# The last eight rows go tile to tile into the first quarter of the columns at two seams

## The chip, the cores and the metric

The kernel runs on one core of one Trainium2 chip. The metric is the device time of one execution in microseconds (us). In the profile PE is the matmul engine (PEld its weight loads), DVE the vector engine, ACT the scalar engine, POOL the GpSimd engine and SP the sync engine, which computes nothing and only issues DMAs. ACT and POOL issue DMAs too; a "q" behind an engine's name (SPq, ACTq) marks its sequencer, which issues and waits.

## The reference

Two layers follow each other. Each normalises a tensor x of 32 images, 48 channels, 64 rows and 128 columns (group norm), and adds to x the result of four scans. In a scan each row (or column) is the input's row plus a convolution of five taps over the row before it, so its steps can't run side by side.

```python
def step(w, b):
    def f(carry, inp):
        nxt = inp + _conv1d(carry, w, b)
        return (nxt, nxt)
    return f
...
x = x + _L0_conv_ref(_gn(x), ...)   # rows down, rows up, columns right, columns left
x = x + _L1_conv_ref(_gn(x), ...)
```

## The kernel before

The 32 images are four groups of eight. A rows phase takes one group through 63 steps down and 63 steps up. A columns phase takes a pair of groups through 127 steps right and 127 left. `PHASES` lists twelve phases, one after the other: eight of rows, four of columns. A step is nine products of matrices on PE (`step`, L741) into three tiles of PSUM, each of which DVE evicts into the big tile `arena` (L750).

The arena holds three slots. In a rows phase the rows 0 to 31 lie in one slot and the rows 32 to 63 in another; a partition is a channel and the column modulo 8. In a columns phase a slot holds a quarter of the columns (32 of them) for both groups of the pair; a partition is a channel and the row modulo 8. So what one row leaves in one partition must go to other partitions, and this goes through DRAM: `move_rows` (L589) writes eight rows to the tensor `upa` or `upb` in ten DMAs, all of whose runs are 32 elements (128 bytes) long, and `load_unit` (L633) reads a sixth of a quarter, in runs of up to 2048 elements.

Where a columns phase follows the rows phase of its own pair (`follows`), the rows leave the last scan just before the columns need them. That is so at two places, here called the seams: from phase 1 to phase 2 and from phase 5 to phase 6. In the upward scan row 0 comes last, and the first quarter of the columns, in the slot that the rows phase leaves free, needs all 64 rows before the first columns step. The second quarter is needed by step 32, the third by step 64, and so on.

The order is written out by hand: `at(t, fn, ...)` puts a call on an agenda at a time counted in steps, and `in_order` chains each engine's instructions in the order in which they were traced. SP issues the DMAs in this order, except those given to another queue. At a seam, with t0 the first step of the columns:

- `plan_rows` cuts the rows into eights, the last eight into two and six (`cuts`, L865 to L868): rows 8 to 15 are written when row 8 is done, rows 2 to 7 when row 2 is done, rows 0 and 1 when row 0 is done.
- `plan_cols` loads the first quarter of the group just scanned on POOL's queue, in five parts of the rows (L897 to L901). The last two parts are rows 2 to 7 and rows 0 and 1.
- `hold_queues` (L648) at t0 + 1.2 makes SP and ACT wait for the first columns step: SP by a DMA of one element of each of the 128 partitions into a DRAM tensor `pin`, ACT by a copy.
- the second quarter is loaded behind it, half of its units on ACT, half on SP (L907), then on SP the third quarter (L910), the spill of the first (L911) and the fourth (L912).

Each DMA of SP and ACT takes the next of eight semaphores in traced order, and waits until the DMA that had this semaphore before, the eighth before it, has landed.

Of the kernel before, what the change touches and what calls it, by code (L numbers as in the profile page):

```python
# [43 lines left out]
E8 = 8  # L44
FULL = 128
NG = E8 * C // FULL
NQ = 4
# [3 lines left out]
PIECES = (  # L51
    (0, 0, 48, 0, 0),
    (1, 0, 48, 0, 48),
    (2, 0, 32, 0, 96),
    (2, 32, 48, 1, 0),
    (3, 0, 48, 1, 16),
    (4, 0, 48, 1, 64),
    (5, 0, 16, 1, 112),
    (6, 0, 48, 2, 0),
# [61 lines left out]
def kernel(  # L121
# [8 lines left out]
    nc = tc.nc  # L130
    B, _, H, W = x.shape
# [5 lines left out]
    RUN = KQ * GB  # L137
# [73 lines left out]
        for half in range(2)  # L211
    }

    def by_row(t, e, h0, h1):


        t = t.rearrange("c (i q a e n) -> e a c i q n", i=E8, q=NQ, a=NH, e=E8)[e, h0 // E8]
        return t[:, h0 % E8 : h0 % E8 + h1 - h0].rearrange("c i q n -> c (i q) n")

    def lines(t, h0, h1):  # L220

# [3 lines left out]
    def by_col(t, e, j):  # L225


        return t.rearrange("c (i q n) -> i q c n", i=E8, q=NQ)[e, j]

    def dma(dst, src, queue=None):  # L230
        (queue or nc.sync).dma_start(dst, src)

    tail = {}

    def in_order(fn, *args):


        traced = nc.cur_bb.bb.instructions
        n = len(traced)
        fn(*args)  # L240
        for ins in traced[n:]:
            if ins.engine in tail:
                tc.add_manual_dep(
                    ins,
                    tail[ins.engine].name,
                    mybir.DependencyInfo(
                        mybir.DependencyClass.NoSync, mybir.DependencyReason.DATA
                    ),
                    reason="in_order",
                )  # L250
            tail[ins.engine] = ins

    def pieces(o):
        return [(e, c0, c1, p0) for e, c0, c1, g, p0 in PIECES if g == o]
# [3 lines left out]
    def slots(k):  # L258

        return (0, 1, 2) if k % 2 == 0 else (2, 1, 0)  # L260
# [322 lines left out]
    def row_views(k):  # L583
        return [slot[i].rearrange("p (o h n) -> p o h n", o=NG, h=HALF) for i in slots(k)]

    def row(k, h):
        return row_views(k)[h // HALF][:, :, h % HALF]

    def move_rows(k, h0, h1, to_dram):  # L589

        _, layer, g = PHASES[k]
        view = row_views(k)[h0 // HALF]
        t = (ups if to_dram else source)[layer][g]
        for h in range(h0, h1, E8):
            end = min(h1, h + E8)
            for o in range(NG):
                for e, c0, c1, p0 in pieces(o):
                    here = view[p0 : p0 + c1 - c0, o, h % HALF : h % HALF + end - h]
                    here = here.rearrange("p h (q n) -> p (h q) n", q=NQ)
                    there = by_row(t, e, h, end)[c0:c1]  # L600
                    if to_dram:
                        dma(there, here)
                    else:
                        dma(here, there)
# [25 lines left out]
    def quarter(k, j):  # L630
        return slot[slots(k)[j % 3]].rearrange("p (o s n) -> p s o n", s=2, o=NG)

    def load_unit(k, j, i, a0=0, a1=NH, e0=0, e1=E8, queue=None):  # L633


        _, layer, pair = PHASES[k]
        o, half = UNITS[i]
        part = slice(a0 * LINE, a1 * LINE)
        for e, c0, c1, p0 in pieces(o):
            if not e0 <= e < e1:  # L640
                continue
            dma(
                quarter(k, j)[p0 : p0 + c1 - c0, half, o, part],
                by_col(ups[layer][2 * pair + half], e, j)[c0:c1, part],
                queue,
            )

    def hold_queues(k):  # L648

        done = quarter(k, 0)[:, 0, 0, RUN : RUN + 1]  # L650
        dma(pin, done)
        nc.scalar.copy(junk[:, BN - 1 :], done)
# [167 lines left out]
    def at(t, fn, *args):  # L820
        agenda.append((t, len(agenda), fn, args))
# [31 lines left out]
    def plan_rows(k, t0, prev):  # L853
        if k == 1:
            ahead, scaled = (-34, -18, -3, 12), (-12, -2, 17, 33)
        elif prev == "cols":
            ahead, scaled = (-28, -12, 4, 20), (-13, 3, 19, 35)
        else:
            ahead, scaled = (-54, -43, 0, 11), (-22, -8, 16, 30)
        if k:  # L860
            for i in range(4):
                at(t0 + ahead[i], move_rows, k, i * LOAD, (i + 1) * LOAD, False)
                at(t0 + scaled[i], scale_rows, k, i * LOAD, (i + 1) * LOAD)

        cuts = list(range(0, H + 1, E8))  # L865
        following = PHASES[k + 1][0] == "cols"
        if following and follows(k + 1):
            cuts = [0, E8 // 4] + cuts[1:]  # L868
        for h0, h1 in zip(cuts, cuts[1:]):
            t = t0 + 2 * (H - 1) - h0  # L870
            if k == 0:
                t += 16 if h0 >= HALF else 68
            elif not following:
                t = t0 + 92 + 5 * (H - h1) / E8 + (34 if h1 <= HALF else 0)
            at(t, move_rows, k, h0, h1, True)
        at(
            t0 + H - 1,
            nc.gpsimd.tensor_copy,
            last.rearrange("p (o n) -> p o n", o=NG),
            row(k, H - 1),  # L880
        )

    def follows(k):

        _, layer, pair = PHASES[k]
        return PHASES[k - 1] == ("rows", layer, 2 * pair + 1)

    def plan_cols(k, t0, prev):
        _, layer, pair = PHASES[k]
        n = 2 * NG  # L890
# [3 lines left out]
        for i in range(n):  # L894
            if follows(k) and UNITS[i][1] == 1:
                other = nc.gpsimd
                at(t0 - 31 + i, load_unit, k, 0, i, 4, NH, 0, E8, other)  # L897
                at(t0 - 13 + i, load_unit, k, 0, i, 2, 4, 0, E8, other)
                at(t0 - 6 + i / n, load_unit, k, 0, i, 1, 2, 0, E8, other)
                at(t0 - 1.5, load_unit, k, 0, i, 0, 1, E8 // 4, E8, other)  # L900
                at(t0, load_unit, k, 0, i, 0, 1, 0, E8 // 4, other)  # L901
            else:
                early = 30 if after else 46 if k == 2 else 70
                at(t0 - early + 2 * i, load_unit, k, 0, i)
            if follows(k):
                queue = nc.scalar if i % 2 else nc.sync
                at(t0 + 1.5, load_unit, k, 1, i, 0, NH, 0, E8, queue)  # L907
            else:
                at(t0 + (3 if after else -24 + 2 * i), load_unit, k, 1, i)
            at(t0 + (38 if after else 8) + 2 * i, load_unit, k, 2, i)  # L910
            at(t0 + 33 + 2 * i, spill_unit, k, i, False)  # L911
            at(t0 + 50 + 2 * i, load_unit, k, 3, i)  # L912
        final = k == len(PHASES) - 1
        left = t0 + W - 1
        end = left + W - 1
        for i in range(n):

            t = left + 64 + 2 * i if layer == 0 else left + 39.5 + 4.5 * i
# [13 lines left out]
        n = len(tiles)  # L932
        direct = [u for u in units if not (final and u[1] == 0)]

        for u, (t, j, i) in enumerate(direct):
            nat = tiles[u % n]
            o, half = UNITS[i]
# [26 lines left out]
        if layer == 0:  # L964
            t = units[-1][0] + 14
# [30 lines left out]
    for k, (kind, layer, _) in enumerate(PHASES):  # L996
        (plan_rows if kind == "rows" else plan_cols)(k, starts[k], PHASES[k - 1][0])
# [26 lines left out]
    def first_group():  # L1024
# [80 lines left out]
        for b in range(GB):  # L1105
            stats.take(NBN // 2, parts[1], b)
            stats.aggregate(b)
        move_rows(0, 8, 16, False)
        for r in range(0, 8, 2):
            permute_rows(1, r, r + 2, free, nc.gpsimd)  # L1110
# [22 lines left out]
        take_in(1, 0, nats1[0])  # L1133

    in_order(first_group)
    at(starts[0] + 10, scale_rows, 0, 40, 48)
    for j in range(1, 4):
# [7 lines left out]
    def catch_up(t):  # L1145
        while agenda and agenda[0][0] <= t:
            _, _, fn, args = agenda.pop(0)
            in_order(fn, *args)

    for k in range(len(PHASES)):  # L1150
        for one in scans(k):
            catch_up(done)
            in_order(one)
            done += 1
# [54 lines left out]
```

## Time and profile before

| | |
|---|---|
| median of three runs | 4293.07 us (4291.05 to 4299.52) |
| the profiled execution's own time | 4290.3 us |
| its span, first to last instruction | 4288.2 us |
| PE busy | 4058.9 us (95%) |
| wait of the first columns step, first seam | 14.1 us |
| the same, second seam | 14.4 us |

The wait rows are from the view of who waited for whom. The steps between them run without a gap on PE, some 1.96 us each, so time is won or lost where PE stops. Other stops (at the start, and at the seam of the two last columns phases) are not touched by the change.

### The profile page before, as it was taken

To read this page: it belongs to the slowest core of one execution; us is meant where nothing else is said; L and a number is where in the kernel's file an instruction comes from. 1 tells how busy PE (TensorE), PEld (TensorE's weight loads), DVE (VectorE), ACT (ScalarE), POOL (GpSimd) and SP (SyncE) were. 2 spreads that over 40 slices of the span, in tenths; PEclk is the share of its full clock that TensorE was granted. 3 is DMA by queue.
4 is the path that set the end of the run, shared out by engine and by line. 5 is a ranking of instruction groups with operands and counts; after the bars stand their busy time and mean duration, and the time that the engine had idled before them with its cause. 6 is when DMAs were issued, how large, how long until landed. Compare 5 with 4: busy or idle time off the path is not lost. (4 is left out here: it accounts for less than half of the span.)

```text
span 4288.2 us, 89979 instructions
## 1 busy us (share of the span) xinstructions
PE 4058.9 (95%) x36648; PEld 4029.3 (94%) x36648; DVE 2164.5 (50%) x6503; ACT 1340.1 (31%) x2662; POOL 886.2 (21%) x906
## 2 busy tenths in 40 slices
PE   3699998999999999998999999999999999999992
PEld 1699998999999999998999999999999999999992
DVE  6345444446664444444446654444444444444443
ACT  1584301435793564100006772613000002210122
POOL 4271001325323020010005310000000024510352
PEclk9899999999999999999999999999999999999996
DMA  9599799857998979679308979939289049999999
GB/s 213 113 216 162 105 167 168 245 127 213 230 198 156 163 140 160 103 127 206 85 1 242 222 154 149 148 50 161 43 140 200 1 78 247 247 243 156 180 202 182
DMA packets 2116733, 680.12 MB, mean 159 GB/s; under 512 B 2005440, under 2 KB 2056160, under 8 KB 2076384
## 3 DMA queue, kind: packets, MB, share of 16 engines
q1 hardware_dynamic: 2015904, 581.64, 70.2%
q10 hardware_dynamic: 97216, 86.44, 9.9%
q0 software_dynamic: 3200, 6.30, 0.5%
q8 instruction: 288, 4.72, 0.5%
q14 instruction: 125, 1.02, 0.1%
HBM read 397.38 MB, written 295.98 MB: 162 GB/s over the span
## 5 line engine op out<-in xcount | busy, mean ns | idle before, releaser
L614 ACT ACTIVATE arena<-arena,offset,scale 128x256 f32<-128x256 f32 (+2 forms) x816 | 575.6, 801 | 432.9 <-DMA arena<-mid 176.1
L673 POOL TENSOR_TENSOR arena<-arena 128x2048 f32<-128x2048 f32 x80 | 363.1, 4553 | 1386.0 <-PE step_10l L741 434.1
L569 POOL COPY arena<-arena 96x256 f32<-96x256 f32 x448 | 265.0, 650 | 553.8 <-DMA arena<-in_x 444.2
L512 ACT ACTIVATE early<-arena 128x256 f32<-128x256 f32 x192 | 129.4, 674 | 477.2 <-POOL arena L673 471.2
L741 PE MATMUL step_00r<-arena,early 128*128 128x128 f32 x2286 | 251.5, 274 | 14.1 <-DMA arena<-upa 14.1
L741 PEld LDWEIGHTS step_00r<-arena,early 128*128 128x128 f32 x2286 | 251.1, 185 | 14.5 <-issue 14.4
L741 PE MATMUL step_01r<-arena,early 128*128 128x128 f32 x2286 | 250.6, 273 | 14.4 <-DMA arena<-upa 14.4
L741 PEld LDWEIGHTS step_01r<-arena,early 128*128 128x128 f32 x2286 | 250.4, 185 | 14.6 <-issue 14.5
L741 PE MATMUL step_11r<-arena,early 128*128 128x128 f32 x2286 | 251.3, 273 | 8.2 <-DVE arena L750 8.2
L741 PEld LDWEIGHTS step_11r<-arena,early 128*128 128x128 f32 x2286 | 250.8, 185 | 8.7 <-DVE arena L750 8.6
L741 PE MATMUL step_00l<-arena,wleft 128*128 128x128 f32 x2286 | 249.1, 272 | 0.0
L741 PEld LDWEIGHTS step_00l<-arena,wleft 128*128 128x128 f32 x2286 | 248.6, 184 | 0.0
L741 PE MATMUL step_10l<-arena,wleft 128*128 128x128 f32 x2286 | 248.5, 272 | 0.0
L741 PE MATMUL step_11l<-arena,wleft 128*128 128x128 f32 x2286 | 248.5, 272 | 0.0
L741 PE MATMUL step_01l<-arena,wleft 128*128 128x128 f32 x2286 | 248.4, 272 | 0.0
L741 PE MATMUL step_10r<-arena,early 128*128 128x128 f32 x2286 | 248.4, 272 | 0.0
L741 PEld LDWEIGHTS step_10l<-arena,wleft 128*128 128x128 f32 x2286 | 248.4, 184 | 0.0
L741 PEld LDWEIGHTS step_11l<-arena,wleft 128*128 128x128 f32 x2286 | 248.4, 184 | 0.0
L741 PEld LDWEIGHTS step_01l<-arena,wleft 128*128 128x128 f32 x2286 | 248.4, 184 | 0.0
L741 PEld LDWEIGHTS step_10r<-arena,early 128*128 128x128 f32 x2286 | 248.4, 184 | 0.0
L698 ACT COPY arena<-arena 128x256 f32<-128x256 f32 x172 | 99.7, 656 | 411.5 <-POOL arena L673 162.2
L240 ACT COPY early<-arena 128x1 f32<-128x1 f32 x2 | 0.4, 191 | 657.9 <-DVE arena L750 657.9
(189 smaller groups left out, 7171.3 us busy)
## 6 DMA issues: line engine op xcount, KB each, us to landing
arena<-in_x SPq DMA_DIRECT2D x24, 1536.0 KB, 11.6
xin<-arena SPq DMA_DIRECT2D x96, 384.0 KB, 4.7
arena<-xin SPq DMA_DIRECT2D x96, 384.0 KB, 8.5
mid<-arena SPq DMA_DIRECT2D x96, 384.0 KB, 7.8
arena<-mid SPq DMA_DIRECT2D x192, 192.0 KB, 4.2
upb<-arena SPq DMA_DIRECT2D x192, 192.0 KB, 3.9
arena<-upb SPq DMA_DIRECT2D x96, 384.0 KB, 12.3
arena<-xin SPq DMA_DIRECT2D x186, 192.0 KB, 4.3
```

What stands on the lines that cost most here:

```text
L240: fn(*args)
L512: nc.scalar.activation(junk[:, 0:n], view[:, b], AF.Identity, accum_out=self.sum[:, i, j : j + 1])
L569: copy(dst[:, r, q], src[:, r0 + r, q])
L614: nc.scalar.activation(args[0], args[0], AF.Identity, bias=args[2], scale=args[1])
L673: eng.tensor_tensor(unit, unit, nat, ALU.add)
L698: copy(by_w(perm)[:, a], src[:, a])
L741: nc.tensor.matmul(part(whole(ps[o])[0:m], -s), weights[:, i, at : at + m], part(src(i), s), start=seen[o] == 1, stop=seen[o] == left[o],)
```

## The change

`send_row` copies one row's first quarter of columns straight from the rows' slot into the first quarter's slot of the columns phase, in one DMA for each piece of the channels that lies together on both sides: 94 DMAs a seam, of 16 to 48 partitions and 128 bytes a partition. They alternate between ACT and SP. For columns 0 to 3 modulo 8 a row is sent when it is done (47 DMAs over eight rows); for columns 4 to 7 all eight rows are sent after the last row, by `send_rest` (47 DMAs). `together` chains these DMAs over the two queues in traced order.

`move_rows` gets a form that writes the first quarter of the columns alone (`nq=1`): this is what goes to DRAM of rows 8 to 15 before the seam. Rows 0 to 7 and 8 to 15 are written in full at t0 + 1.3, which is behind `hold_queues` and ahead of the loads of the second quarter. The loads of rows 0 to 7 by POOL fall away.

```diff
+    def send_row(k, h, wanted):
+        here = row(k - 1, h)
+        for e, c0, c1, o, p0 in PIECES:
+            if e not in wanted:
+                continue
+            for i, d0, d1, to, q0 in PIECES:
+                a, b = max(c0, d0), min(c1, d1)
+                if i != h or a >= b:
+                    continue
+                turns[0] += 1
+                dma(
+                    quarter(k, 0)[q0 + a - d0 : q0 + b - d0, 1, to, e * RUN : (e + 1) * RUN],
+                    here[p0 + a - c0 : p0 + b - c0, o, 0:RUN],
+                    nc.scalar if turns[0] % 2 else nc.sync,
+                )
+
+    def send_rest(k, wanted):
+        for e in wanted:
+            for h in range(E8 - 1, -1, -1):
+                send_row(k, h, (e,))
+
+    together += [send_row, send_rest]
...
-        if following and follows(k + 1):
-            cuts = [0, E8 // 4] + cuts[1:]
+        seam = following and follows(k + 1)
+        if seam:
+            cuts = cuts[2:]
+            end = t0 + 2 * (H - 1)
+            at(end - E8, move_rows, k, E8, 2 * E8, True, 1)
+            for h in range(E8 - 1, -1, -1):
+                at(end - h, send_row, k + 1, h, range(0, E8 // 2))
+            at(end, send_rest, k + 1, range(E8 // 2, E8))
+            at(end + 1.3, move_rows, k, 0, E8, True)
+            at(end + 1.3, move_rows, k, E8, 2 * E8, True)
...
-                at(t0 - 1.5, load_unit, k, 0, i, 0, 1, E8 // 4, E8, other)
-                at(t0, load_unit, k, 0, i, 0, 1, 0, E8 // 4, other)
```

More of the change, by code (lines that the diff above doesn't have):

```diff
@@ L212, with by_row @@
     }
-    def by_row(t, e, h0, h1):
+    def by_row(t, e, h0, h1, nq):
         t = t.rearrange("c (i q a e n) -> e a c i q n", i=E8, q=NQ, a=NH, e=E8)[e, h0 // E8]
-        return t[:, h0 % E8 : h0 % E8 + h1 - h0].rearrange("c i q n -> c (i q) n")
+        t = t[:, h0 % E8 : h0 % E8 + h1 - h0]
+        return t.rearrange("c i q n -> c (i q) n") if nq == NQ else t[:, :, 0]
     def lines(t, h0, h1):
@@ L233 @@
     tail = {}
+    queues = (nc.sync.engine, nc.scalar.engine)
+    together = []
     def in_order(fn, *args):
@@ L250, in in_order @@
                 )
+            if ins.engine in queues and "DMA" in ins.opcode:
+                if fn in together and "queue" in tail:
+                    tc.add_manual_dep(
+                        ins,
+                        tail["queue"].name,
+                        mybir.DependencyInfo(
+                            mybir.DependencyClass.NoSync, mybir.DependencyReason.DATA
+                        ),
+                        reason="together",
+                    )
+                tail["queue"] = ins
             tail[ins.engine] = ins
@@ L587, in row, with move_rows @@
         return row_views(k)[h // HALF][:, :, h % HALF]
-    def move_rows(k, h0, h1, to_dram):
+    def move_rows(k, h0, h1, to_dram, nq=NQ):
         _, layer, g = PHASES[k]
@@ L598, in move_rows @@
                     here = view[p0 : p0 + c1 - c0, o, h % HALF : h % HALF + end - h]
-                    here = here.rearrange("p h (q n) -> p (h q) n", q=NQ)
-                    there = by_row(t, e, h, end)[c0:c1]
+                    there = by_row(t, e, h, end, nq)[c0:c1]
+                    if nq == NQ:
+                        here = here.rearrange("p h (q n) -> p (h q) n", q=NQ)
+                    else:
+                        here = here[:, :, 0:RUN]
                     if to_dram:
@@ L646, in load_unit @@
             )
+    turns = [0]
+    def send_row(k, h, wanted):
[12 more added lines that the diff above has]
+                    nc.scalar if turns[0] % 2 else nc.sync,
+                )
+    def send_rest(k, wanted):
[3 more added lines that the diff above has]
+    together += [send_row, send_rest]
     def hold_queues(k):
```

## The prediction

> **What bounds the kernel now.** PE is busy 95% of the span, so I went to the view of who waited for whom on PE and took the waits that the change can reach:
>
> ```profile
> PE step_01r L741 <- DMA arena<-upa: 14.4, 1, 14.4
> PE step_00r L741 <- DMA arena<-upa: 14.1, 1, 14.1
> ```
>
> Each is one wait, the first columns step at a seam. The timeline of the first seam shows what it waits for:
>
> ```profile
> 654.44 5.16 SPq L231 DMA_DIRECT2D upa<-arena  x10
> 657.50 3.94 POOL L231 DMA_DIRECT2D arena<-upa  x8 [3.22 <-DMA upa<-arena]
> 662.19 1.00 POOL L231 DMA_DIRECT2D arena<-upa  x2 [0.74 <-issue]
> 665.29 24.97 PE L741 MATMUL step_00r<-arena,early 128*128 128x128 f32 x200 [14.10 <-DMA arena<-upa]
> 668.34 0.35 SPq L231 DMA_DIRECT2D pin<-arena  x1
> 668.77 19.67 ACTq L231 DMA_DIRECT2D arena<-upa  x6
> 668.78 20.10 SPq L231 DMA_DIRECT2D arena<-upa  x6
> ```
>
> The last row's eviction ends at 651.59 (call this T). Its write starts only at 654.44, since SP still issues rows 2 to 7; the loads by POOL run till 664.7. Then SP sends the pin DMA, and both queues start on the second quarter. Step 1's last eviction ends at 670.01, that is T + 18.42, where an ordinary step takes 1.96. Of the 16.46 lost, 14.10 is PE idle and 2.36 is the slow clock behind it. The busy time by stretches shows that clock, and something else:
>
> ```profile
> 654.00:665.00 11.00, 0.00 (x0) 0.00 (x0) 0.00 (x0) 0.00 (x0) 5.22 (x11) 0.50 0.63 115
> 665.00:671.00 6.00, 5.71 (x27) 5.58 (x27) 1.05 (x3) 0.19 (x1) 0.00 (x0) 0.50 0.73 21
> 671.00:677.00 6.00, 6.00 (x58) 6.00 (x57) 2.88 (x9) 0.00 (x0) 0.00 (x0) 1.00 0.69 31
> 677.00:717.00 40.00, 39.98 (x369) 39.91 (x368) 19.66 (x62) 0.00 (x0) 0.00 (x0) 1.00 0.98 171
> ```
>
> The last three columns are granted clock, DMA share and GB/s. From 668 to 676 the DMA engines are held but move 21 to 31 GB/s, against 171 later. That stretch is the pin DMA's life; the list of issues has it at 8.1 us to landing for half a kilobyte:
>
> ```profile
> pin<-arena SPq DMA_DIRECT2D x1, 0.5 KB, 8.1
> ```
>
> At the second seam pin is issued at 1946.31 and 8 KB packets become short again at 1954.8: the same 8.5. I read it as 128 writes of 4 bytes to one place that hold up all that is behind them.
>
> The second quarter's loads end at 716.7 (last issue 703.6, 12.9 to landing); at the second seam at 1990.2. They are needed by step 32, DVE's row with the longer 0.65:
>
> ```profile
> 730.25 0.65 DVE L750 SCALAR_TENSOR_TENSOR arena<-step_00r,bd,arena 128x128 f32<-128x128 f32 x2 [0.72 <-PE step_00r L741]
> 731.14 0.35 DVE L750 SCALAR_TENSOR_TENSOR arena<-step_00r,bd,arena 128x128 f32<-128x128 f32 x1 [0.23 <-PE step_00r L741]
> ```
>
> So step 32 ends at 731.49 = T + 79.9, with 14 us of slack on its loads. At the second seam T is 1929.35 and step 32 ends at 2008.63, T + 79.3, with 17 us of slack. The change eats this slack from both ends: the steps come earlier, the loads later. Last, the price of 128-byte packets, from the DMA view of 618 to 630, where rows are written and little else runs:
>
> ```profile
> DMA packets 14970, 1.95 MB, mean 162 GB/s; under 512 B 14959, under 2 KB 14959, under 8 KB 14969
> q1 hardware_dynamic: 14952, 1.89, 100.7%
> ```
>
> 14952 packets in 12 us at a full share: 1246 packets per us.
>
> **What goes at the start of the columns.** The write and read of rows 0 to 7 leave the path. Row 0's five pieces for columns 0 to 3 are issued within 1 to 2 us of T. Tile-to-tile copies are not in this trace; the nearest rows are the smallest row writes here, at 1.6 to 2.0 from issue to landing, as an upper end the 4.0 of a 192 KB row write. I take 1.8, since these pieces are smaller than either. Step 1 then starts near T + 1.5 to 3 in place of T + 13.7, and step 32 would end near T + 65 if nothing else held it: 15 us better. The pieces for columns 4 to 7 land in the order in which steps 4 to 7 want them; the worst is 1 or 2 us late. The added waits on PE's first eight steps are some tenths each. All this is hidden if step 32 stalls anyway, so the next part decides.
>
> **What comes on the path: the second quarter.** Its loads read whole channels of the group just scanned, so they must follow the full write of rows 0 to 15, which now stands behind hold_queues, which stands behind 47 pieces on SP. Queued behind the same writes: on ACT its ten loads (its statistics start only at 728.2, and wait for an input load that is late too); on SP the other ten, the third quarter, an input load, the spills. Counted from T at the first seam:
> - Send_rest: 47 pieces on two queues, 24 on one. SP's ten issues in 5.16 us are 0.52 each: 12.5, starting 0.6 after T. Pin is issued at T + 13.1. If the eight semaphores bind instead, with 4.0 to landing, it is 47 x 4.0 / 8 = 23.5; with the 1.8 taken they don't (10.6).
> - Pin holds the engines for 8.1: T + 21.2. Bounds: nothing, if 128-byte writes pass where 8 KB reads did not, and 8.5. I take all of it, as both queues stood still under it at both seams.
> - Two blocks of rows, 8 x 384 x 4 x 2 = 24576 packets at 1246 per us: 19.7. T + 40.9. The last landing 2.0 later (1.6 to 4.0): T + 42.9. In the trace of before most of this ran ahead of the seam, beside row steps.
> - The loads: before they took from pin's landing at 676.4 to 716.7, 40.3, and 1.2 for what had passed under pin: 41.5. T + 84.4. Bounds: 31.3, if 6.29 MB go at the 201 GB/s of 710 to 720, and 45.
> - Step 32's evictions 1.0: T + 85.4. It has waited over 20 us, so I add the slow clock behind such a wait, 2.4 as at the seam: T + 87.8.
>
> Against T + 79.9 that is 7.9 lost. At the second seam the loads took 1954.8 to 1990.2, with 1.2 for the rest 36.6: 42.9 + 36.6 + 3.4 = T + 82.9 against T + 79.3, 3.6 lost. Together 11.5. The first quarter of rows 8 to 15 written twice is within these packets; written ahead it is 3072 packets, 2.5 us in a stretch that now has room, at no cost on PE while POOL's loads of these rows end before T (they take 5 us of the 16). SP's later work starts about 17 us later; the fourth quarter's loads at the first seam landed at 832, 28 before use, so I count nothing there.
>
> The profiled execution took 4290.3, its span 4288.2, the median is 4293.07. 4290.3 + 11.5 = 4301.8; the median carried over gives 4304.6, and I say 4304. About 0.2%, 8.6 us, is what a measurement of this kernel can tell from no change.
>
> **Two rules beside the rows.** The Trainium skill, "TensorE: Matmul & The Clock Gate", section "Part 1: The HAM clock gate", has the full clock back after some 3.4 us of sustained work, where the row shows half clock for 5.7 us after PE resumed; by the rule the term would be 1.7, the total 1.4 us less. The Trainium skill, "DMA: Bandwidth & Descriptors", section "Bandwidth", advises against just such small pieces (below 64 KB the descriptors dominate), and its section "Anatomy of one DMA" has a fixed 2.0 us for each; an estimate from that page is 47 x 2.0 / 8 = 11.8 in place of 12.5. No run here shows such a piece yet.
>
> **The rivals.**
> - *Pin holds nothing back.* [...] Against: even the other queue's packets stood. Each seam is 8.1 better, together 11.5 - 16.2 = -4.7: 4288, no change to be told.
> - *Faster: the second quarter comes in time.* If pin holds nothing and the loads run at 201 GB/s, the seams come to T + 66.1 + 3.4 = 69.5: 10.4 and 9.8 won, 4273. From loads landed by about T + 64 on, the whole 14 to 15 a seam is won: 4264. For: alone on the engines, loads do reach that rate at 710. Against: 159 to 184 GB/s from 680 to 710 with two queues reading, as here.
> - *Slower still: the pieces bind.* With 4.0 to landing, 11 more a seam: 4326. For: the writes beside full engines show it. Against: the engines are nearly idle just then.
>
> That the chain over two queues does not hold is hardly open: in the built program ACT and SP each have 47 pieces, in turn, and pin behind them.
>
> **How the numbers follow.** Forecast 0.52, pin holds nothing 0.20, faster 0.20, pieces bind 0.08. The forecast's own bounds (issue at 0.44 instead of 0.52, loads 3 either way, landing) are about 9 either way, 4295 to 4313, and reach into "same" with a tenth; the second case spreads into "faster" a little. So slower 0.54, same 0.23, faster 0.23. The range 4272 to 4322 leaves out the full gain and the worst of the last case.
>
> **What would show it.** Right: PE's wait of 14 gone or under 4 at the seams, and in its place one wait of 15 to 25 at step 32, on DMA arena<-upa; ACT's ten loads issued from T + 43; few GB/s in the 8 us behind pin. Wrong: no wait at step 32 (the gain stands), writes at full rate right behind pin (second case), or pin issued after T + 20 (last case).

## The result, and the profile after

The changed kernel takes 4316.9 us (median of five, 4310.94 to 4323.94), beside 4294.43 for the kernel before (4291.05 to 4299.52): a ratio of 1.0051, 95% interval 1.0035 to 1.0066. It is slower by some 22 us, twice what was forecast. Its profiled execution took 4312.47, with a span of 4310.7.

Again the view of who waited for whom on PE comes first (in all, times, longest):

```profile
PE step_00r L785 <- DVE arena L794: 17.2, 2, 16.3
PE step_01r L785 <- DVE arena L794: 15.9, 2, 14.0
PE step_00r L785 <- DMA arena<-arena: 6.5, 2, 5.4
PE step_01r L785 <- DMA arena<-arena: 6.2, 1, 6.2
```

The wait of 14 at the first step has become one of 5.4 and 6.2 on the pieces, `arena<-arena`. A new one of 16.3 and 14.0 stands at step 32. It names DVE, not a DMA, since PE waits for the eviction of step 32 and DVE waits for the loads. The timeline of the first seam says so, and gives the chain (T, the end of row 0's eviction, is 641.86 here):

```profile
639.47 23.09 ACTq L232 DMA_DIRECT2D arena<-arena  x34
640.00 23.50 SPq L232 DMA_DIRECT2D arena<-arena  x35
646.89 14.13 PE L785 MATMUL step_00r<-arena,early 128*128 128x128 f32 x108 [5.42 <-DMA arena<-arena]
663.60 0.53 SPq L232 DMA_DIRECT2D pin<-arena  x1
664.17 25.59 SPq L232 DMA_DIRECT2D upa<-arena  x20
692.89 25.87 ACTq L232 DMA_DIRECT2D arena<-upa  x10
730.48 0.61 DVE L794 SCALAR_TENSOR_TENSOR arena<-step_00r,bd,arena 128x128 f32<-128x128 f32 x2 [16.58 <-DMA arena<-upa]
730.89 9.28 PE L785 MATMUL step_00r<-arena,early 128*128 128x128 f32 x62 [16.26 <-DVE arena L794]
```

Each line hands on to the next: pieces until 663, then pin, behind it the twenty writes of rows 0 to 15, behind these ACT's ten loads (the last lands at 730.26, and DVE's 0.61 is step 32's eviction). The busy time of the four stretches between these points, with granted clock, DMA share and GB/s in the last three columns:

```profile
641.86:663.60 21.74, 15.61 (x122) 15.11 (x123) 5.68 (x18) 0.19 (x1) 0.00 (x0) 0.84 0.10 13
663.60:671.40 7.80, 6.88 (x63) 6.69 (x62) 3.40 (x11) 0.00 (x0) 0.00 (x0) 1.00 0.75 54
671.40:692.80 21.40, 21.40 (x199) 21.40 (x199) 10.58 (x33) 0.00 (x0) 0.00 (x0) 1.00 0.89 142
692.80:730.26 37.46, 21.82 (x201) 21.63 (x200) 10.31 (x32) 0.00 (x0) 0.00 (x0) 0.85 1.02 194
```

In the first stretch the DMA engines are one tenth busy: 22 us go by in which two queues issue small DMAs. In the second, pin's, 54 GB/s get through: over 7.8 us that is some 3,300 of the 24,576 packets of 128 bytes that wait behind pin. In the third stretch the writes run, in the fourth the loads.

Everything below counts from T, and a seam is measured from T to the end of step 127. That was 265.63 and 265.00 before and is 277.84 and 277.93 after: 12.2 and 12.9 lost, 25.1 together. The rest of the two profiled spans differs by 2.7 the other way: 9.7 less ahead of the first seam, 7.0 more between the seams, neither in a place that the change touches. Among the profiles below these two parts move by up to 15 and 12 us with no order in it, so the seams say more than single times do.

### The profile page after: what moved, and what is told of

It is laid out like the page before. It is cut to its first block, busy times and chain, and to the rows that moved or that the text cites. A ratio compares the mean times of both kernels' runs of the same rounds, so it can differ in the third digit from the quotient of the medians.

```text
span 4310.7 us, 90284 instructions
## 1 busy us (share of the span) xinstructions
PE 4069.0 (94%) x36648; PEld 4037.3 (94%) x36648; DVE 2146.3 (50%) x6503; ACT 1340.1 (31%) x2662; POOL 881.7 (20%) x886
## 5 line engine op out<-in xcount | busy, mean ns | idle before, releaser
L785 PEld LDWEIGHTS step_01r<-arena,early 128*128 128x128 f32 x2286 | 255.1, 188 | 22.8 <-DVE arena L794 16.3
## 6 DMA issues: line engine op xcount, KB each, us to landing
arena<-upb SPq DMA_DIRECT2D x96, 384.0 KB, 12.5
```

What stands on the lines that cost most here:

```text
L785: nc.tensor.matmul(part(whole(ps[o])[0:m], -s), weights[:, i, at : at + m], part(src(i), s), start=seen[o] == 1, stop=seen[o] == left[o],)
```

## The experiments

All edits are to the changed kernel where nothing else is said. The runs went in three groups, each beside the kernel before on its own chip (medians 4293.85, 4293.56 and 4295.51). Most of what they gave is in this table; "first" is the wait of the first columns step, "32" the end of step 32 from T, and a seam is T to step 127.

| | us | ratio to before, 95% | first | 32 | seams |
|---|---|---|---|---|---|
| before | 4294.43 | | 14.1, 14.4 | 79.9, 79.3 | 265.6, 265.0 |
| changed | 4316.9 | 1.0051 (1.0035 to 1.0066) | 5.4, 6.2 | 89.2, 90.0 | 277.8, 277.9 |
| no pin | 4304.03 | 1.0021 (1.0012 to 1.0030) | 5.5, 6.3 | 83.1, 80.0 | 270.8, 268.1 |
| pin apart | 4309.63 | 1.0033 (1.0021 to 1.0045) | 5.5, 6.2 | 82.9, 83.2 | 270.9, 271.4 |
| pieces on SP | 4373.37 | 1.0182 (1.0166 to 1.0197) | 18.0, 19.7 | 114.7, 118.0 | 302.5, 305.7 |
| pieces on three queues | 4298.15 | 1.0014 (1.0006 to 1.0023) | 3.1, 4.0 | 75.9, 80.9 | 264.2, 269.7 |
| rows 8 to 15 ahead | 4308.72 | 1.0035 (1.0024 to 1.0046) | 10.8, 11.1 | 80.9, 83.3 | 270.0, 269.3 |
| second quarter first | 4299.05 | 1.0010 (0.9999 to 1.0021) | 6.1, 5.8 | 73.5, 75.4 | 278.4, 261.1 |
| the same, no pin, two queues | 4283.87 | 0.9981 (0.9973 to 0.9989) | 5.8, 6.3 | 72.2, 73.9 | 259.5, 259.6 |
| the same, three queues | 4272.42 | 0.9953 (0.9941 to 0.9965) | 4.1, 4.3 | 68.9, 69.7 | 254.6, 255.5 |
| before, no pin | 4306.43 | 1.0032 (1.0020 to 1.0045) | 22.4, 22.3 | 87.0, 86.7 | 272.7, 272.4 |

**Without the pin DMA.** ACT is still held by its copy.

```diff
-        dma(pin, done)
```

> The changed kernel with the pin DMA left out of hold_queues: SP goes straight from its last piece to the writes of rows 0 to 15. Theory (the second quarter's chain sets step 32, and pin is 8 us of it): writes start at T + 22 and land at T + 43 instead of T + 51, step 32 ends at T + 81 instead of T + 89 at both seams, the wait there falls from 16 and 14 to about 8 and 6; 16 us less than the changed kernel, some 6 us more than the kernel before. Rival (pin only waits beside other work, 128-byte writes pass it): writes land where they did, nothing changes. Rival (the cost sits in the first steps, not at step 32): nothing changes either.

Step 32 ends 6.1 and 9.9 earlier, the seams are 7.0 and 9.8 shorter. So pin does hold back the writes behind it: they have landed at T + 45.0 and T + 44.7, in place of T + 50.9 and T + 49.7. These 5.9 and 5.0 are less than pin's own 8 us, since some writes pass while it lasts. The rest of the gain at the second seam is in the loads, which took 34.4 there in place of 39.5; no run says why. Step 32 still waits, and the kernel is still no faster than before: pin is one term of the loss, not all of it.

**The pin DMA to places 4 KB apart.** This asks what the 8 us are.

```diff
-    pin = dram.tile([FULL, 1], ...)
+    pin = dram.tile([FULL, 1024], ...)[:, 0:1]
```

> The changed kernel with the pin DMA's 128 elements written 4 KB apart in DRAM, not one behind the other. Theory: its 8 us are 128 writes of 4 bytes that queue up at one place of DRAM; apart they land in 2 to 3 us, the writes behind them run at once, step 32 ends about T + 83 and T + 80 as without the pin DMA, and the time is about 4304 to 4306. Rival: each write of 4 bytes costs its 63 ns wherever it goes; pin lands in 8 us again, 4317.

The list of issues of the changed kernel and that of this one, the last number the median from issue to landing:

```profile
pin<-arena SPq DMA_DIRECT2D x2, 0.5 KB, 7.8
```

```profile
pin<-arena SPq DMA_DIRECT2D x2, 0.5 KB, 2.0
```

The same 128 writes of 4 bytes take 2.0 in place of 7.8, and the rows behind them land 5.4 and 5.0 earlier, much as without pin. What costs is that the writes lie side by side in 512 bytes, not their number or size; distances between 4 bytes and 4 KB were not tried. The Trainium skill, "DMA: Bandwidth & Descriptors", section "Specifications", says that below 512 bytes the DMA engines read, change and write back. That alone, these rows show, is not dear: apart, each write is just as small. The cost comes when many of them lie together.

**All pieces on SP, and pieces on three queues.** Both ask what the pieces cost: the issue on a queue, or the landing.

```diff
-                    nc.scalar if turns[0] % 2 else nc.sync,
+                    nc.sync,                                              # one
+                    (nc.sync, nc.scalar, nc.gpsimd)[turns[0] % 3],        # three
```

> The changed kernel with all 94 pieces of a seam on SP's queue, none on ACT's. What it measures is the issue cost: in the changed kernel each queue issues a piece every 0.64 us, both together one every 0.32. If the two queues share what limits them, one queue alone issues one every 0.32 to 0.35 and nothing else moves. If 0.6 is what an issue costs on any queue, the second half of the pieces takes 47 x 0.6 = 28 us instead of 15, pin goes out at T + 36 or later, the steps 5 to 8 wait, and step 32 ends at T + 103: 28 us more than the changed kernel. I expect between: an issue alone at 0.5, pin at T + 30, 17 us more.

> The changed kernel with the 94 pieces of a seam dealt to three queues in turn, SP, ACT and POOL. On SP alone an issue took 0.63 us, on each of two queues 0.64: the issue itself costs that, the queues don't share it. Theory (the issue cost sets when pin and the writes go out, and this sets step 32): about 0.21 each over three queues, 0.5 on POOL; pin at T + 15 to 16 instead of T + 21.7, the first step's wait 3 to 4 instead of 5.4 and 6.2, step 32 at T + 83 instead of T + 89; 12 us less than the changed kernel. Rival (the landings or the engines limit the pieces): pin stays near T + 21, no gain.

On one queue the pieces follow each other every 0.63 us, on two every 0.32 over both, so 0.64 on each; the landing stays at 1.7 to 1.8 (medians). The cost belongs to the queue that issues, and the second queue really halves it. On one queue pin is issued at T + 49.1 and T + 51.1 in place of T + 21.7, and the seams are 24.7 and 27.8 longer, more than expected: at T, 76 and 79 of the 94 pieces were still to be issued. On three, POOL takes 0.50 per piece, pin is issued at T + 10.3 and T + 10.9, and the seams are 13.6 and 8.2 shorter, though a piece now lands in 2.4 to 2.7 (medians of the queues). What is won at the second seam is less than the 10.8 by which pin came sooner; step 32 still waits there for 12.3, for DVE and so for the loads. The Trainium skill, "DMA: Bandwidth & Descriptors", section "Issuing engines are not separate DMA queues", says that issuing from several engines saves the time on the sequencer alone, "which is usually small relative to the DMA itself". Here it isn't small: of a piece's 0.64 on the queue and 1.8 to landing, the first is paid 47 times in a row and the second once.

**Rows 8 to 15 in full ahead of the seam.** Half of the late writes are gone.

```diff
-            at(end - E8, move_rows, k, E8, 2 * E8, True, 1)
+            at(end - E8, move_rows, k, E8, 2 * E8, True)
-            at(end + 1.3, move_rows, k, E8, 2 * E8, True)
```

> The changed kernel with rows 8 to 15 written in full ahead of the seam, as in the kernel before, and only rows 0 to 7 written behind the hold. By the volume alone 12288 packets, 10 us, leave the path at each seam: step 32 at T + 79, 20 us less in all. Against it: SP issues these ten writes ahead of the pieces, at 1.2 us each when the engines are full, till about T - 5, and the pieces then land in 3 to 4 us instead of 1.7, so eight in flight give 0.45 instead of 0.32 each: the first step starts at T + 10 or later and pin goes out at T + 28 instead of T + 22. My theory expects this to eat most of the gain: step 32 at T + 84 to 88, the time between the changed kernel and 10 us less.

Half of it came as expected: ten late writes, the last landing at T + 44.8 and T + 47.2. Step 32 ends at T + 80.9 and T + 83.3, somewhat sooner than expected. But the last piece goes out only at T + 25.8 at both seams, in place of T + 21.1 and T + 20.7, and the first step waits 10.8 and 11.1. The pieces didn't land late, as the theory had it (1.77, as before). SP's first piece went out at T - 5.5 and T - 5.8, behind the ten larger writes, in place of T - 11.2 and T - 9.7, and at T it had 39 and 40 pieces left. Such a backlog doesn't melt: six pieces a row on two queues take 1.9 us, and a row takes 1.96.

**The second quarter's part first.** Loads of the second quarter need only that quarter of the late rows.

```diff
-            at(end + 1.3, move_rows, k, 0, E8, True)
-            at(end + 1.3, move_rows, k, E8, 2 * E8, True)
+            for h in (0, E8):
+                at(end + 1.3, move_rows, k, h, h + E8, True, (1, 2))
+            for h in (0, E8):
+                at(end + 1.6, move_rows, k, h, h + E8, True, (2, 3))
+                at(end + 30, move_rows, k, h, h + E8, True, (3, NQ))
```

(The last argument is a range of quarters. In this one run the fourth quarter's part of rows 0 to 15 is written after its slot has been loaded with the third quarter, so these values are not the reference's; the amount of work is the same.)

> The changed kernel, pin kept, but behind it only the second quarter of the columns of rows 0 to 15 is written before the second quarter's loads (6144 packets in 20 DMAs instead of 24576); the third quarter's part is written behind these loads, the fourth's later, the first's not again. Theory (the volume written ahead of the loads is on the path): 6144 packets are 5 us, but 20 issues at 0.5 are 10, so the writes land near T + 40 instead of T + 51, the loads at T + 77, step 32 ends at T + 77 to 79, the wait there is 1 to 4; about 22 us less than the changed kernel, so within 5 us of the kernel before. Rival (the loads are held by something else, such as the queues' semaphores): step 32 stays at T + 86 or later.

The loads of ACT start at T + 39.0 and T + 40.6 in place of T + 51.0 and T + 50.2, and step 32 hardly waits (0.8 at the first seam, nothing at the second). The first seam ought to have been the shortest so far. It isn't, for a wait that the changed kernel doesn't have:

```profile
PE step_00r L787 <- DMA xin<-arena: 16.4, 1, 16.4
```

It stands at step 96. The row's name is that of the DMA which released the semaphore last; by its place it is the fourth quarter's loads, which land at T + 215, behind the part that SP now writes at T + 119 to T + 139. That this part is what makes them late is argued, not shown. The second seam has no such wait and is 16.8 shorter than in the changed kernel.

**The same without pin, on two queues; and with the pieces on three.** The parts of the second quarter are dealt to SP and ACT, the third's and fourth's written by SP and ACT behind the loads and before the slot is loaded anew.

```diff
-        dma(pin, done)
...
+            for h, queue in ((0, nc.sync), (E8, nc.scalar)):
+                at(end + 1.3, move_rows, k, h, h + E8, True, (1, 2), (queue,))
+            for q, queue in ((2, nc.sync), (3, nc.scalar)):
+                for h in (0, E8):
+                    at(end + 1.6, move_rows, k, h, h + E8, True, (q, q + 1), (queue,))
```

> The changed kernel without pin, with the second quarter's part of rows 0 to 15 written first, ten DMAs on SP and ten on ACT, then the loads of the second quarter, then the third quarter's part on SP and the fourth's on ACT, all before those rows are overwritten; the first quarter's part of rows 0 to 7 is not written, nobody reads it. Theory: writes land at T + 29, loads at T + 66, before step 32 wants them at T + 73; no wait there. SP's queue is 20 DMAs shorter than where the second quarter alone went first, so the fourth quarter's loads, 16 us late there at the first seam, come in time or a few us late. Both seams end about 4 to 6 us earlier than in the kernel before: 8 to 12 us less than it. Rival (moving writes behind the seam only moves the wait to the next quarters): a wait of 10 or more at step 64 or 96, no gain.

> The kernel that sends the second quarter's part first and has no pin DMA (4283.9), with the pieces dealt to SP, ACT and POOL. Theory: the pieces end 9 to 10 us earlier, the first step's wait falls from 5.8 and 6.3 to about 3.2 and 4.0, step 32 still doesn't wait: 2.5 less a seam, about 4279. Rival: POOL's loads of rows 8 to 15 and its pieces stand in each other's way, the first step starts as late as before or later, 4284 to 4290.

The first beats both kernels: loads landed at T + 64, no wait at step 32, the seams 6.1 and 5.4 shorter than before. At step 96, with less on SP's queue, 1.0 is left of the 16.4. The second adds the line with three queues of above, and is the fastest found: 4272.42, a ratio of 0.9953. Of all the waits of above only these are left:

```profile
PE step_01r L789 <- DMA arena<-arena: 4.3, 1, 4.3
PE step_00r L789 <- DMA arena<-arena: 4.1, 1, 4.1
```

The waits fell by 1.7 and 2.0 from the two-queue form, the seams by 4.9 and 4.2: with the pieces done by T + 11, the smaller waits behind the first step are gone too.

**Fewer pieces ahead, and the order over both queues.** From the two-queue form: rows 8 to 15 written by SP and ACT in turn ahead of the seam, and only columns 0 to 2 sent row by row.

```diff
-            at(end - E8, move_rows, k, E8, 2 * E8, True, (0, 1))
+            at(end - E8, move_rows, k, E8, 2 * E8, True, (0, 1), (nc.sync, nc.scalar))
-                at(end - h, send_row, k + 1, h, range(0, E8 // 2))
-            at(end, send_rest, k + 1, range(E8 // 2, E8))
+                at(end - h, send_row, k + 1, h, range(0, 3))
+            at(end, send_rest, k + 1, range(3, E8))
```

> As the kernel with the second quarter first, no pin and the rest on both queues, and besides: the ten writes of rows 8 to 15 ahead of the seam alternate between SP and ACT, and only the columns 0 to 2 modulo 8 are sent row by row, 3 to 7 behind row 0. Theory (the first step waits 5 to 6 us because the pieces of rows 7 to 0 start behind these writes and just keep pace with the rows, 5.9 pieces at 0.32 against 1.97 a row): the pieces catch up, row 0's go out at once, the first step's wait falls to 2 to 3, and step 32, held by nothing, comes 3 to 4 us earlier at each seam: 6 to 8 us less than without this. Rival (the wait is the landing of the last row's pieces alone): 1 us or nothing.

4419.64, a ratio of 1.0294 (1.0281 to 1.0308), some 136 us more than the form that it was made from. The first step waits 81.4 and 62.7. Ahead of the first seam (T is 651.68) SP issues nothing for 94 us, from 542.56 to 636.86. The queue waits name what it stood for, and the timeline shows what ended it:

```profile
SPq L234 <- DMA upa<-arena: 208.9, 23, 96.5
```

```profile
635.07 2.36 ACTq L234 DMA_DIRECT2D upa<-arena  x5
636.86 19.43 SPq L234 DMA_DIRECT2D upa<-arena  x20
```

SP waited 96.5 for a write that ACT had to issue: ACT's first, of 635.07, landed at 636.79, and SP's next DMA, which takes the same semaphore, went out at 636.86. Each DMA takes the next of eight semaphores in the order over both queues, and ACT's five writes had been put into that order long before their row was done, so SP stood still for one of them. Two more runs ask whether that is so: one takes the chain off the pieces in the changed kernel, one puts ACT's writes into the chain.

```diff
-    together += [send_row, send_rest]                     # the first
+    together += [send_row, send_rest, move_turns]         # the second: move_turns calls move_rows
```

> The changed kernel without the chain of the pieces over the two queues (each queue keeps its own order; only the place that a piece has in the order over both queues, and with it its semaphore, is free). Theory: the eight semaphores are dealt out in the order over both queues, so without the chain SP's earlier writes wait for a semaphore that an ACT piece holds which can't start before its row is done; SP stands still for tens of us ahead of the seam, the first columns step starts 20 to 80 us late at each seam, 4350 to 4450 in all. Rival: the order on each queue is all that counts, 4317 as the changed kernel.

> The kernel of the run that took 4420 (rows 8 to 15 written by SP and ACT in turn ahead of the seam, columns 0 to 2 alone sent row by row), with these writes chained over both queues too. Theory: the 80 us of that run were SP waiting for a semaphore of ACT's writes that stood too early in the order over both queues; chained, SP doesn't stand still, the first step waits 4 to 6, and the time is 4280 to 4290. Rival: ACT as a writer, or column 3 sent late, costs it by itself: 4350 or more.

Without the chain 4493.62 (two runs), a ratio of 1.0465 (1.0445 to 1.0484), though each queue issues the same DMAs in the same order as the changed kernel. The first step waits 107.6 and 86.8, more than expected. The queue waits show the same stop, now for the pieces:

```profile
SPq L232 <- DMA arena<-arena: 240.2, 16, 99.8
```

With the writes chained 4281.07, a ratio of 0.9974 (0.9964 to 0.9983), seams of 258.1 and 257.9, and no such wait on SP. So the order over both queues is what the 136 us were, and what the chain of this change is for. What was left of the edit's aim also shows: the first step waits 1.4 and 1.8 in place of 5.8 and 6.3, but of the columns sent after the last row, now five, one comes late and costs a wait of 2.9 a seam, at T + 12.5 and T + 12.0. The seams are 1.4 and 1.7 shorter than in the two-queue form, where 3 to 4 were expected.

**The kernel before without its pin DMA.** The last question is what pin is for.

```diff
-        dma(pin, done)                                     # in the kernel before
```

> The kernel before, with the pin DMA left out: SP is not held, ACT is. What it measures: whether pin is what slows the loads for 8 us behind the first step. Theory: 8 KB packets take under 1 us from the start, the second quarter's loads end 8 us or more sooner, and the time is unchanged within 0.1%, since step 32 had 14 and 17 us of slack. Rival (the slow stretch is the loads' own start): packets of 3 to 5 us for the first 8 us as before.

It is slower by 13, where no change was expected: the first step waits 22.4 and 22.3. The view of one tile has POOL's last ten loads of the first seam, in the kernel before and in this one:

```profile
DMA to landing us min/median/max: 2.0/2.0/2.5
```

```profile
DMA to landing us min/median/max: 2.1/4.1/10.1
```

They are issued at T + 5.8 to T + 11.3, and SP, no longer held, issues its loads of the second quarter from T + 8.1. So POOL's small loads, for which the first step waits, take up to 10.1 to land beside SP's, and the last has landed at T + 21.4 in place of T + 13.2. The question itself is answered too: in the first 8 us of SP's loads 203 GB/s move, where it was 37 beside pin, and the second quarter has landed at T + 52 at both seams in place of T + 65 and T + 61. Pin does slow the loads, but it pays for itself there. In the changed kernel those loads of POOL are gone, and with them the reason to hold SP.

## Why the prediction was right, and where its sizes were off

- **The direction and its cause.** Slower, because the first step's gain is given back at step 32, where the second quarter comes too late. The profile has both, in the order foretold, and the runs with the second quarter's part first show it: where the loads come in time, the wait at step 32 is gone. Of the signs, the wait at step 32 came as 16.3 and 14.0, where 15 to 25 was written.
- **The issue of the pieces: the step that failed.** The forecast had 24 issues of 0.52 on SP from T on, pin at T + 13.1. Pin went out at T + 21.7 at both seams, 8.6 later. At T, SP still had 31 and 33 pieces to issue, not 24: SP's first piece left at T - 11.2 and T - 9.7, behind the ten writes of rows 8 to 15, where row 7 is done at T - 13.7, and the pieces of the rows behind it queued up. And a piece takes 0.64 on its queue, not the 0.52 of a row write. 33 x 0.64 is 21.1, and 0.6 for the last is T + 21.7 at the second seam; at the first it is 31 x 0.64 = 19.8, with a pause of 1.3 more, whose cause stays open.
- **Landing, and the rival "the pieces bind".** The text named pin after T + 20 as the sign of this rival, and that sign came. But its mechanism did not: landing is 1.8, as taken, and not the 4.0 of that case. What binds is the issue. The fixed 2.0 us that the prediction cites beside this is given in that section for DMAs issued from GpSimd; these go out from SP and ACT. The result, 4316.9, lies 12.9 above the forecast and 9.1 below this rival's 4326. That is 3.9 above the forecast's own bounds, 4295 to 4313, and inside the stated range because the range takes in part of the rivals' cases.
- **Pin.** 8.1 was taken; it landed in 7.7 and 8.0. The rival in which it holds nothing back is ruled out: without pin the writes land 5.9 and 5.0 earlier, with pin apart 5.4 and 5.0. But the prediction took it to hold everything back, and some writes pass.
- **The writes.** 19.7 and 2.0 for the last landing were taken; from pin's landing it took 21.5 and 20.0 till all had landed. This agreement is luck in part: some packets had passed under pin, and without pin the same writes take 23.6 and 24.1 from the first issue.
- **The loads.** 41.5 and 36.6 were taken; they took 37.5 and 39.5. The slow clock behind step 32 cost 2.5 and 2.2, beside 2.4. The errors of the loads, 4.0 too much and 2.9 too little, are of opposite sign and almost cancel; that too is luck.
- **The first step.** Foretold near T + 1.5 to 3, it starts at T + 5.0 and T + 5.8, for the same backlog of pieces; PE's wait was 5.4 and 6.2 where "under 4" was written. Step 32 hides that.
- **The sum.** 7.9 and 3.6 foretold, 12.2 and 12.9 found. The 13.6 between them are twice 8.6 of late pin, less 3.6 that the other terms give back.
- **The gain of the first step**, the faster rival, exists, but not in full: with the second quarter's loads landed at T + 58 and T + 53 the fastest form wins 11.0 and 9.6 a seam, not 14 to 15, since its first step still waits 4.1 and 4.3. The point from which it was to decide, loads landed by about T + 64, isn't tested: the two-queue form landed at T + 64 and doesn't wait, but its step 32 ends only at T + 72.2 and T + 73.9.

## What to carry to other kernels

Count a row of small DMAs by what the queue needs for each, not by landing or bytes, and count the backlog at the moment that matters too. When a wait is taken off the path, look for what stood in the same queue behind it: here a barrier and full rewrites that had been free before. And where queues share semaphores, the order over all queues is part of the program: a DMA put too early on a quiet queue stops the busy one.

## What the hardware showed that was not expected

- 128 writes of 4 bytes into one stretch of 512 bytes of DRAM take 7.8 us to land, 4 KB apart 2.0. Side by side they also hold up what is queued behind them: 37 GB/s of loads beside them in the kernel before, 203 without them, and 5 to 6 us at the late writes of the changed kernel.
- A tile-to-tile DMA of 2 to 6 KB costs its queue 0.64 us on SP or ACT and 0.50 on POOL. Two queues issue side by side without slowing each other, and a DMA lands in 1.8; with three queues it lands in 2.3 to 2.7.
- A small load of POOL that lands in 2.0 takes up to 10.1 when SP starts large loads beside it.
